# W_v's block differences: formed in advance through device memory, or in their places when these fall free

## The chip, the cores and the metric

The kernel runs on one core of one Trainium2 chip. The metric is the device time of one launch in microseconds (us), as the median of several runs. TensorE (PE in the profile; PEld its weight loads), VectorE (DVE), ScalarE (ACT), GpSimd (POOL) and SyncE (SP) work side by side, each through its own queue in order. SP, ACT and POOL also issue DMAs (SPq, ACTq, POOLq in the timelines).

## The reference

One pre-normed graph-attention layer on 2708 nodes with 1024 features, all in float32:

```
h   = relu(layernorm(x))
q   = h @ W_q.T + b_q;   k = h @ W_k.T + b_k;   v = h @ W_v.T + b_v
z   = (q @ k.T) / sqrt(1024) * adj            # adj: 0 or 1, about 4 ones in a row
z   = where(z == 0, -10000, z)
out = x + relu(softmax(z, axis=1) @ v)
```

## The kernel before

The weights of q and k are multiplied into one matrix first, so that a score is a row of h times a row of `h @ M`. Each node has few neighbours, so scores and sums go over gathered rows of h and not over whole rows of adj. W_v is applied last, to the weighted sums of h.

**Two big products, one after the other.** Both are [2708 x 1024] by [1024 x 1024]: first h by the joined matrix (the q units), then the weighted sums u by W_v (the o units). Rows come in 22 tiles of 128, two tiles in a *unit*. There are ten q units (numbers 0 to 9, the last is `last_q`) and ten o units from 10 on; one tile stays alone at the end. A unit is a 2 x 2 block product in seven block products instead of eight (`multiply`, L1063): on the right stand the 512 x 512 blocks of the matrix, three of them used as they are, and four differences. The blocks lie in `M[:, i, j]`, [128, 4, 512] each, and the differences in `T[:, 0..3]`, the same shape, inside the tile `wlow`:

```
T0 = M01 - M00    T1 = M11 - T0    T2 = M11 - M01    T3 = M10 - T1
```

The order of a unit's products on TensorE is: s2 T1, a12 M10, s4 M11, s3 T2, then for the next unit a11 M00 and s1 T0, then a22 T3. `M[:, 0, 1]` (M01) is used in differences alone. The left factors a and s are sums and differences of the unit's row blocks. For the o units VectorE turns the rows (L706) and makes s1 and s3 (L723, L743); GpSimd makes s2 and s4 (also L723). Each product is eight matmul records of 128x512 in the trace, about 3.4 us.

**Steps of a unit.** `after(i)`, i from 0 to 6, is called between the products of unit n; (n, i) names the place. What is written there is put into the program at that point. VectorE's queue keeps exactly this order from unit 4 (`FIRST`) on; the queues of ScalarE, SyncE and GpSimd are ordered by the framework's scheduler from then on. Each `after` also runs the attention stream a little further (`advance`).

**The attention stream** (`attention`) takes tile after tile. For a tile with K neighbours a row: GpSimd gathers K buffers of 128 rows of h (L611), each 128x1024; its query rows `pq` are loaded (L851, or gathered, L613); VectorE makes K scores (`junk`, L881); ScalarE takes the exponential; VectorE makes the weights (`coef`, `w`, `m`); ScalarE starts the sum `u` with the first buffer (L930, L921), VectorE adds the others (L941, L947), and each step frees its buffer for a later gather. The sum goes to `u_dram` (through `v`, L962) and comes back as rows `or` of an o unit (L701). Buffers are handed out from the list `free` in order. There are eleven buffers `slots` and, as two more, the place of M01. A gather leaves out the rows of missing neighbours, so a buffer must hold finite numbers before its first use.

**Where the results of a q unit go.** `q_results` copies or adds the banks into q (ScalarE L1107, L1118; VectorE L1113, L1110) and stores q (L1103). In an o unit the additions are L1144 and L1140.

**W_v's way in.** At (3, 4), `searched` loads W_v's four blocks into `slots[0..7]`, in sixteen pieces of 256 KB (L802). At (4, 1) and (4, 5), `ts_of_wv` forms the four differences with sixteen subtractions of 128x512 (L811 to L814) and stores them to `tv_dram` with sixteen DMAs (L816). At (4, 6) those eight buffers join the free list. In units 9 and 10, as each place falls free of the joined matrix, seven loads of 1 MB on SyncE's queue bring M00, T0, T1, M10, M11, T2 and T3 (L1335):

```
for k, at in enumerate(((0, 0), (0, 1), (0, 3), (0, 4), (0, 5), (0, 5), (1, 2))):
```

Each pair is (n - last_q, i).

## Time and profile before

| | |
|---|---|
| time, median of 3 runs | 655.42 us (654.75 to 655.88) |
| the profiled execution | 654.23 us, span 652.5 us |
| TensorE / VectorE busy | 631.6 us (97%) / 525.0 us (80%) |
| GpSimd / ScalarE busy | 403.1 us (62%) / 281.6 us (43%) |
| moved by DMA | 187.46 MB, 287 GB/s over the span |
| granted TensorE clock, mean | 0.991 |

A timeline row gives the start from the beginning of the span, the time taken (of a whole run of equal instructions, x their number), engine, line, operation, out<-in, the shape, and in brackets how long the engine stood idle before it and what ended that. A window row gives the busy time of each engine in a stretch, with the granted clock, the busy share of the DMA engines and their rate. `wlow` stands for a T, `M` for a block or, in a gather, for its use as a buffer; `psy`, `ps` are banks of results.

### The profile page before, as it was taken

The page shows a single profiled execution, that of the slowest core. Times are in us where ns is not written, and L with a number is a line of the kernel's source. Part 1 is how long each engine was busy: PE and PEld are TensorE (multiplying, and loading weights), DVE is VectorE, ACT ScalarE, POOL GpSimd, SP SyncE. Part 2 cuts the span into 40 slices and gives each one's busy share as a digit, 9 for nine tenths or more (in the row PEclk, how much of TensorE's full clock was granted, in tenths as well). Part 3 has the DMA queues.
Part 4 walks back from the last instruction along what each step waited for, and adds up shares of the span by engine and source line. Part 5 has one row for each costly group of instructions (what it writes and reads, how often), then busy time and mean ns, then how long its engine had stood idle before and what let it go on. Part 6 is the DMA issues. An engine that isn't in the chain of part 4 may idle for free.

```text
span 652.5 us, 6269 instructions
## 1 busy us (share of the span) xinstructions
PE 631.6 (97%) x1651; PEld 318.5 (49%) x1651; DVE 525.0 (80%) x988; ACT 281.6 (43%) x423; POOL 403.1 (62%) x415
## 2 busy tenths in 40 slices
PE   9999999999989999999999987999999999999994
PEld 5777766444434444444444432444444444444441
DVE  5999788998893754989879927999998898998521
ACT  3548974948495532434422132443233233342300
POOL 2549950976847677776752812677868787874421
PEclk9999999999999999999999997999999999999998
DMA  8998988597789969996799998999999989982551
GB/s 337 406 353 313 357 317 325 174 367 273 249 300 348 344 191 403 336 323 187 240 317 354 255 417 235 285 307 350 330 358 334 322 242 283 260 274 64 136 167 57
DMA packets 65089, 187.46 MB, mean 287 GB/s; under 512 B 10343, under 2 KB 15799, under 8 KB 64152
## 3 DMA queue, kind: packets, MB, share of 16 engines
q1 hardware_dynamic: 34410, 89.10, 39.6%
q0 software_dynamic: 25136, 78.41, 38.1%
q10 hardware_dynamic: 5502, 19.48, 7.6%
q8 instruction: 15, 0.25, 0.2%
q14 instruction: 26, 0.21, 0.1%
HBM read 151.94 MB, written 44.93 MB: 302 GB/s over the span
## 4 chain that ended last, share of the span: by engine, by line
PE 58%; DMA 13%; DVE 13%; issue 8%; POOL 4%; ACT 2%; another core or an unknown queue 0%; POOLq 0%; DVEq 0%; SPq 0%; ACTq 0%
PE ps L1029 23%; PE psy L1029 16%; DMA g<-h_dram,tab 7%; PE ps_y L477 6%; DVE u L941 5%; DVE junk L881 4%; PE ps_x L477 4%; PE ps_z L477 4%; PE pt L416 3%; DMA y<-in_x_dram,tab 2%; POOL g L611 2%; DMA h_dram<-x 2%; DMA qr<-h_dram,tab 1%; DMA M<-in_wv_dram 1%; ACT sized L369 1%
## 5 line engine op out<-in xcount | busy, mean ns | idle before, releaser
L1029 PE MATMUL psy<-wlow,s 128*128 128x512 f32 x320 | 144.2, 593 | 3.5 <-ACT psy L1042 1.9
L1029 PE MATMUL ps<-M,a 128*128 128x512 f32 x320 | 144.2, 593 | 0.5 <-ACT ps L761 0.5
L611 POOL DMA_INDIRECT g<-h_dram,tab x87 | 105.1, 1207 | 44.9 <-issue 18.0
L881 DVE SCALAR_TENSOR_TENSOR junk<-g,pq 128x1024 uint8<-128x1024 f32 x86 | 110.5, 1285 | 22.5 <-DMA pq<-q_late 14.4
L941 DVE SCALAR_TENSOR_TENSOR u<-g,coef,u 128x1024 f32<-128x1024 f32 x67 | 94.3, 1408 | 3.9 <-ACT u L930 2.4
L1029 PEld LDWEIGHTS psy<-wlow,s 128*128 128x128 f32 x320 | 59.3, 190 | 73.5 <-issue 68.6
L1029 PEld LDWEIGHTS ps<-M,a 128*128 128x128 f32 x320 | 59.6, 190 | 71.3 <-issue 68.1
L1029 PE MATMUL ps<-wlow,s 128*128 128x512 f32 x160 | 74.7, 611 | 4.5 <-DVE s L723 4.5
L390 DVE FIND_INDEX8 at<-ones,adj 128x8 uint32<-128x685 f32 (+1 forms) x88 | 74.5, 865 | 0.0
L1029 PE MATMUL ps<-M,s 128*128 128x512 f32 x160 | 72.0, 593 | 0.9 <-DMA M<-in_wv_dram 0.9
L1029 PE MATMUL psy<-wlow,a 128*128 128x512 f32 x160 | 71.9, 592 | 0.0
L369 ACT ACTIVATE sized<-adj 128x2708 uint8<-128x2708 f32 (+1 forms) x22 | 54.2, 2466 | 7.4 <-DMA adj<-in_adj_dram 6.1
L299 POOL TENSOR_TENSOR hsum<-hsum,x 128x256 f32<-128x256 f32 (+1 forms) x56 | 38.6, 730 | 27.4 <-DVE wlow L445 23.5
L1029 PEld LDWEIGHTS ps<-wlow,s 128*128 128x128 f32 x160 | 31.2, 196 | 44.9 <-issue 43.5
L1029 PEld LDWEIGHTS ps<-M,s 128*128 128x128 f32 x160 | 30.2, 190 | 39.3 <-issue 38.8
L1029 PEld LDWEIGHTS psy<-wlow,a 128*128 128x128 f32 x160 | 30.4, 190 | 38.3 <-issue 37.8
L1128 POOL DMA_INDIRECT y<-in_x_dram,tab x19 | 33.1, 1740 | 17.7 <-ACT y L1145 8.0
L723 POOL TENSOR_TENSOR s<-s,a 128x512 f32<-128x512 f32 x18 | 24.2, 1346 | 30.9 <-DVE s L723 30.7
L826 POOL DMA_INDIRECT out_dram<-y,tab x21 | 28.7, 1368 | 20.6 <-DMA y<-in_x_dram,tab 8.2
L930 ACT ACTIVATE u<-g,coef 128x1024 f32<-128x1024 f32 x15 | 17.2, 1150 | 37.6 <-DVE coef L929 33.5
L723 POOL TENSOR_TENSOR s<-a,s 128x512 f32<-128x512 f32 x18 | 29.6, 1646 | 1.2
L627 POOL DMA_INDIRECT tab_dram<-tab,pos_i x22 | 22.2, 1008 | 11.8 <-DVE pos_i L690 6.3
(254 smaller groups left out, 899.2 us busy)
## 6 DMA issues: line engine op xcount, KB each, us to landing
adj<-in_adj_dram SPq DMA_DIRECT2D x21, 1354.0 KB
x<-in_x_dram SPq DMA_DIRECT2D x21, 512.0 KB
h_dram<-x ACTq DMA_DIRECT2D x21, 512.0 KB
q_late<-q SPq DMA_DIRECT2D x12, 512.0 KB
pq<-q_late SPq DMA_DIRECT2D x12, 512.0 KB
u_dram<-v ACTq DMA_DIRECT2D x10, 512.0 KB
or<-u_dram SPq DMA_DIRECT2D x40, 128.0 KB
g<-in_wv_dram SPq DMA_DIRECT2D x16, 256.0 KB
```

The source lines that it names most:

```text
L299: small.append(nc.gpsimd.tensor_add(hsum[:n, cols], hsum[:n, cols], xt[:n, cols]))
L369: nc.scalar.activation(sized[:n], a[:n, :, :PW], AF.Abs, accum_out=total[:n, t:t + 1])
L390: nc.vector.max_index(at[:n, k - first_k, g, :], ones[:n, 0:8], a[:n, g, :])
L477: mm = nc.tensor.matmul(bank, a_tile(o + H * a[0], a[1], i), b(o), start=first and o == 0, stop=(o == H - 1), skip_group_check=True)
L611: return nc.gpsimd.indirect_dma_start(out=dst, out_offset=None, in_=src, in_offset=off, bounds_check=N - 1, oob_is_err=False)
L627: put = nc.gpsimd.indirect_dma_start(out=tab_dram[lo >= EARLY][:, :], out_offset=bass.IndirectOffsetOnAxis(ap=pos_i[:n, t:t + 1], axis=0), ...
L723: step = (eng or nc.vector).tensor_tensor(ops[name], a, b, op=op)
L826: to = nc.gpsimd.indirect_dma_start(out=out, out_offset=bass.IndirectOffsetOnAxis(ap=ptab.bitcast(U32)[:n, t, SLOTS:SLOTS + 1], axis=0), i ...
L881: chained(lambda: nc.vector.scalar_tensor_tensor(junk, g_of[t][s], 1.0, tq[t], op0=ALU.mult, op1=ALU.mult, accum_out=zall[:, t, s:s + 1]))
L941: chained(lambda: nc.vector.scalar_tensor_tensor(u, g_of[t][s], coef[:, s:s + 1], u, op0=ALU.mult, op1=ALU.add))
L1029: mm = nc.tensor.matmul(bank, a[:, c, :], b[:, c, :], start=False, stop=(c == 3), skip_group_check=True)
L1128: return nc.gpsimd.indirect_dma_start(out=y[:n], out_offset=None, in_=x, in_offset=off, compute_op=ALU.add)
```

## The change

The differences are no longer made in advance. `slots` are not loaded with W_v; at (4, 1) VectorE sets eight of them to zero (the other three are cleared on GpSimd as before), and all eleven join the free list before the first gathers. M01's place holds W_v's second block from (8, 0) on, and joins the free list, as two buffers, only at (10, 1). Five loads of 1 MB remain: M01 at (8, 0), M00 at (9, 0), the block M11 into T1's place at (9, 2), M10 at (9, 3) and M11 at (9, 4). Four subtractions of 128x2048 on VectorE make T0 at (9, 2), T1 in its own place at (9, 5), T3 at (10, 0) and T2 at (10, 1).

```diff
-    tv_dram = dram.tile([4, P, 4, NB], FT, name="tv_dram")
...
-        for c in range(4):
-            for k, (i, j) in enumerate(((0, 0), (0, 1), (1, 1), (1, 0))):
-                nc.sync.dma_start(slots[2 * c + k // 2][:, k % 2 * NB:(k % 2 + 1) * NB], wv[j][:, i * 4 + c, :])
         assert len(adj_loads) == NT
-        free.extend([M.rearrange("p i j (a c) w -> p i j a (c w)", a=2)[:, 0, 1, a, :] for a in range(2)] + slots[8:])
-
-    def ts_of_wv(lo, hi):
-        with tc.issue_after(behind[-1].ins), tc.issue_after(sorted_at[-1].ins):
-            for c in range(lo, hi):
-                b11, b12 = slots[2 * c][:, :NB], slots[2 * c][:, NB:]
-                b22, b21 = slots[2 * c + 1][:, :NB], slots[2 * c + 1][:, NB:]
-                nc.vector.tensor_sub(b11, b12, b11)
-                nc.vector.tensor_sub(b12, b22, b12)
-                nc.vector.tensor_sub(b22, b22, b11)
-                nc.vector.tensor_sub(b21, b21, b22)
-                for k, r in enumerate((b11, b22, b12, b21)):
-                    nc.sync.dma_start(tv_dram[k][:, c, :], r)
...
     def attention(order):
         for t in order[:2]:
             ask(t)
+        free.extend(slots)
...
         marked(0, EARLY)
-        free.extend(slots[:8])
-        fill()
...
-            if (n, i) in ((FIRST, 1), (FIRST, 5)):
-                ts_of_wv(i // 2, i // 2 + 2)
+            if (n, i) == (FIRST, 1):
+                for g in slots[:HIGH - 3]:
+                    nc.vector.memset(g, 0.0)
+            b11, b12, b21, b22 = M[:, 0, 0], M[:, 0, 1], M[:, 1, 0], M[:, 1, 1]
+            for at, place, src in (((-1, 0), b12, of_wv(0, 1)), ((0, 0), b11, of_wv(0, 0)), ((0, 2), T[:, 1], of_wv(1, 1)),
+                                   ((0, 3), b21, of_wv(1, 0)), ((0, 4), b22, of_wv(1, 1))):
+                if (n - last_q, i) == at:
+                    nc.sync.dma_start(place, src)
+            for at, place, a, b in (((0, 2), T[:, 0], b12, b11), ((0, 5), T[:, 1], T[:, 1], T[:, 0]),
+                                    ((1, 0), T[:, 3], b21, T[:, 1]), ((1, 1), T[:, 2], b22, b12)):
+                if (n - last_q, i) == at:
+                    nc.vector.tensor_sub(place, a, b)
+            if (n - last_q, i) == (1, 1):
+                free.extend(M.rearrange("p i j (a c) w -> p i j a (c w)", a=2)[:, 0, 1, a, :] for a in range(2))
...
-            for k, at in enumerate(((0, 0), (0, 1), (0, 3), (0, 4), (0, 5), (0, 5), (1, 2))):
-                if (n - last_q, i) == at:
-                    place, src = ((M[:, 0, 0], of_wv(0, 0)), (T[:, 0], tv_dram[0]), (T[:, 1], tv_dram[1]),
-                                  (M[:, 1, 0], of_wv(1, 0)), (M[:, 1, 1], of_wv(1, 1)), (T[:, 2], tv_dram[2]),
-                                  (T[:, 3], tv_dram[3]))[k]
-                    nc.sync.dma_start(place, src)
```

## The prediction

> **What bounds it now.** I read the page first, then the windows by stretch, then TensorE's timeline for its pauses, and the other engines' timelines around the longest pause.
>
> ```profile
> span 652.5 us, 6269 instructions
> PE 631.6 (97%) x1651; PEld 318.5 (49%) x1651; DVE 525.0 (80%) x988; ACT 281.6 (43%) x423; POOL 403.1 (62%) x415
> ...
> 187.00:205.00 18.00, 15.04 (x35) 6.19 (x33) 13.05 (x30) 13.96 (x16) 11.42 (x17) 1.00 1.02 387
> 205.00:230.00 25.00, 24.48 (x83) 12.81 (x84) 14.87 (x44) 13.78 (x26) 18.55 (x30) 1.00 0.91 317
> ...
> 376.00:400.00 24.00, 17.76 (x41) 7.23 (x40) 8.80 (x17) 5.96 (x11) 1.34 (x3) 0.96 1.03 386
> 400.00:410.00 10.00, 10.00 (x18) 4.30 (x19) 9.37 (x17) 4.15 (x9) 5.54 (x4) 0.75 0.61 140
> 410.00:434.00 24.00, 24.00 (x57) 10.61 (x57) 23.54 (x38) 9.91 (x16) 15.84 (x12) 1.00 1.02 302
> ```
>
> The page gives TensorE 631.6 of 652.5 us. The window rows (busy time of PE, PEld, DVE, ACT, POOL, then granted clock, DMA share, GB/s) say where the rest is. In 376 to 400 TensorE is busy 17.76 of 24 us and VectorE only 8.80, while the DMA engines are full (share 1.03, 386 GB/s); the next 10 us run at a granted clock of 0.75. From 410 on VectorE is busy 23.54 of 24 us. So TensorE sets the pace wherever its inputs are there, VectorE is just behind it, and this one hole is made by transfers. TensorE's timeline has its pauses:
>
> ```profile
> 193.34 3.70 PE L1029 MATMUL psy<-wlow,s 128*128 128x512 f32 x8 [1.87 <-ACT psy L1042]
> ...
> 205.52 1.06 PE L416 MATMUL pt<-ident,qr 128*128 128x128 f32 x8 [1.60 <-DMA qr<-h_dram,tab]
> ...
> 372.40 3.60 PE L1029 MATMUL psy<-wlow,a 128*128 128x512 f32 x8
> ...
> 383.77 3.67 PE L1029 MATMUL ps<-M,s 128*128 128x512 f32 x8 [0.91 <-DMA M<-in_wv_dram]
> 388.27 3.67 PE L1029 MATMUL psy<-wlow,s 128*128 128x512 f32 x8 [0.83 <-DMA wlow<-tv_dram]
> 391.78 3.60 PE L1029 MATMUL ps<-M,a 128*128 128x512 f32 x8
> 399.88 6.25 PE L1029 MATMUL ps<-wlow,s 128*128 128x512 f32 x8 [4.50 <-DVE s L723]
> ...
> 426.56 3.60 PE L1029 MATMUL ps<-wlow,s 128*128 128x512 f32 x8
> ```
>
> Four pauses lie in what the change touches: 1.60 at 205.52 for rows read back from h_dram, 0.91 at 383.77 for a block of W_v, 0.83 at 388.27 for a stored difference, and 4.50 at 399.88 for VectorE's s. The group after the last one takes 6.25 us where its neighbours take 3.60, so that pause costs 4.50 + 2.65 = 7.15 us. Why s was late stands in VectorE's timeline:
>
> ```profile
> 368.22 0.68 DVE L1110 TENSOR_TENSOR q<-psy,p 128x512 f32<-128x512 f32 x1
> ...
> 378.35 1.18 DVE L881 SCALAR_TENSOR_TENSOR junk<-M,pq 128x1024 uint8<-128x1024 f32 x1
> ...
> 379.46 1.28 DVE L941 SCALAR_TENSOR_TENSOR u<-g,coef,u 128x1024 f32<-128x1024 f32 x1
> 395.19 1.23 DVE L881 SCALAR_TENSOR_TENSOR junk<-g,pq 128x1024 uint8<-128x1024 f32 x1 [14.44 <-DMA pq<-q_late]
> ...
> 399.04 0.69 DVE L723 TENSOR_TENSOR s<-a,s 128x512 f32<-128x512 f32 x1
> ...
> 423.11 0.69 DVE L723 TENSOR_TENSOR s<-a,s 128x512 f32<-128x512 f32 x1
> ```
>
> VectorE ended its work at 380.74 (379.46 + 1.28), stood still for 14.44 us until the query rows pq of the next tile had landed, and only then came to s (395.19 to TensorE's restart at 399.88: 4.69 us). SyncE's queue shows what lay ahead of those rows:
>
> ```profile
> 345.37 0.37 SPq L1335 DMA_DIRECT2D M<-in_wv_dram  x1
> 348.56 0.32 SPq L1335 DMA_DIRECT2D wlow<-tv_dram  x1
> ...
> 355.43 0.32 SPq L1335 DMA_DIRECT2D wlow<-tv_dram  x1
> ...
> 367.11 2.64 SPq L1335 DMA_DIRECT2D M<-in_wv_dram  x2
> 370.57 0.33 SPq L1335 DMA_DIRECT2D wlow<-tv_dram  x1
> 371.23 7.99 SPq L1103 DMA_DIRECT2D q_late<-q  x2
> ...
> 379.32 0.44 SPq L851 DMA_DIRECT2D pq<-q_late  x1
> ```
>
> In order: M's first block, T0, T1, the third and fourth block, T2, two stores of q, and pq, issued at 379.32 and used at 395.19, 15.87 us later; T3 follows right behind. Seven transfers of 1 MB belong to W_v.
>
> **Part by part.** The costs come from these rows:
>
> ```profile
> g<-in_wv_dram SPq DMA_DIRECT2D x6, 256.0 KB
> ...
> wlow<-tv_dram SPq DMA_DIRECT2D x4, 1024.0 KB
> ...
> L812 DVE TENSOR_TENSOR g<-g,g x4: 691/691/692, 224.5 to 241.6; 128x512 f32<-128x512 f32 x4
> ...
> L445 DVE TENSOR_TENSOR wlow<-M x4: 1204/1218/1220, 93.0 to 113.0; 128x1024 f32<-128x1024 f32 x4
> ...
> L141 DVE MEMSET keys<- 128x352 f32 x1 | 0.4, 352 | 1.0 <-PEq L1558 1.0
> ```
>
> The early part, units 3 and 4. Sixteen loads of 256 KB and as many stores go. Six of the loads are issued from 187 to 205; at 387 GB/s these 1.57 MB are 4.1 us of the DMA engines' time, in the stretch in which TensorE waits 1.60 us for its rows. I take the whole 1.60 (bounds: 0, if those rows lose their time to the store of h_dram ahead of them, and 1.60). The sixteen small subtractions (0.69 us) go from VectorE, and eight memsets of 128x1024 come. No row has that shape; 128x352 takes 352 ns, so by proportion about 1.0 us each, 8 us in place of the 5.5 of the first eight subtractions. VectorE is busy 14.87 of 25 us there, so both are hidden; were they not, it would be 2.5 us.
>
> The gather buffers fall from 13 to 11 from unit 4 until unit 10, since M's fourth block now waits in its place. I price that at nothing in the forecast and return to it as a rival.
>
> Units 8 to 10. Of the seven 1 MB loads, T0, T2 and T3 are gone, T1's place takes a block of W_v instead, and the block that waits in M comes a unit earlier: four remain around the hole and one ahead of it. That one joins SyncE's queue behind unit 7's stores; it has no reader to wait for, since its place is no gather buffer any more. VectorE gets four subtractions of 128x2048. From 512 to 1024 columns the time grows by 1218 - 691 = 527 ns, so 2048 columns take about 1218 + 2 x 527 = 2.27 us, 9.1 in all. VectorE is on no spare time here, so all four move what comes behind them in its queue. T0's and T1's come before 378.35, T3's before the weights ahead of it, T2's just before the junk at 378.35. Their inputs: M's first block was issued at 345.37, T1's at 355.43, the third and fourth at 367.11, each over 10 us before the subtraction that needs it, so I count no wait (bound: 1 us for the last, for which TensorE itself waited 0.91). Behind T0's stands the addition of 368.22, which must read a bank before TensorE's group of 372.40 adds to it: it ends at 368.90 + 2.27 = 371.2, with 1.2 us to spare.
>
> Is a product held up? T0, T1 and T3 are ready ahead of theirs. T2 is ready at 378.35 + 4 x 2.27 = 387.4. Without its two small pauses TensorE would be there at 388.27 - 0.91 - 0.83 = 386.5, so it waits 0.9 and reaches s at 391.78 + 3.60 - 388.27 + 387.4 = 394.5.
>
> When does VectorE go on? It gets to the pq wait at 380.74 + 9.1 = 389.8. If pq still landed at 395.19 the subtractions would all fit in the old wait. With T2's megabyte gone from ahead of pq in the same queue it lands 1.05 MB / 386 GB/s = 2.7 us sooner, 392.5; with T0's and T2's both, 389.8. T0 was issued 31 us earlier and is long through, so I take 392.5 and keep 389.8 and 395.2 as ends. TensorE then restarts at 392.5 + 4.69 = 397.2, 2.7 us sooner, after a pause of 2.7 us in place of 4.50.
>
> The clock decides 2.65 us more. After the pause of 1.87 at 193.34 the next group took 3.70, after 4.50 it took 6.25. 2.7 is nearer to the first, so I count the 2.65 as gained. Then TensorE is 2.65 us nearer to VectorE: the next s ended at 423.80 (423.11 + 0.69) and was used at 426.56, 2.76 us later, which just covers it. [...]
>
> Sum: 1.60 + 2.7 + 2.65 = 6.9 us. The profiled execution took 654.23 us (its span and 1.73 around it) and becomes 647.3; the median shown is 655.42, 1.19 above it, so the prediction for a median is 648.5. With pq at 389.8 it is 9.6 us, 645.8.
>
> **The rivals.**
>
> ```profile
> 377.25 1.15 ACT L921 ACTIVATE u<-hsum,m 128x1024 f32<-128x1024 f32 x1 [0.80 <-DVE m L920]
> 378.30 0.57 ACT L1118 COPY q<-psy 128x512 f32<-128x512 f32 x1
> ...
> 380.78 1.04 ACT L962 COPY v<-u 128x1024 f32<-128x1024 f32 x1 [1.29 <-DVE u L941]
> 381.73 0.58 ACT L1073 COPY u<-psy 128x512 f32<-128x512 f32 x1
> ```
>
> *Queues behind the weights (slower).* ScalarE copies the last q (L1118, 378.30) behind u (L921), which needs VectorE's weights; SyncE stores that q and only then issues pq. T0's, T1's and T3's subtractions now come before those weights, so the copy, the store and pq's issue all move by 6.8 us, pq to 386.1. If it again took 15.87 us less the 2.7 of T2, it would land at 399.3, 4.1 us later than before; TensorE restarts at 404.0 at a low clock, and the time is 655.42 + 4.1 - 1.60 = 657.9. It decides for slower once pq takes over 395.19 - 386.1 = 9.1 us. For it: the order of those two queues in the trace. Against it: by 386 the third and fourth block have landed, so little is queued ahead; and both queues are ordered anew around the subtractions. [...]
>
> *The copy of u2 behind v (faster by less).* v (L962, 380.78) follows VectorE's u of 379.46, and u2 (L1073) stands behind it; TensorE may write that bank with T2's product only after u2. Moved by 9.1 us, v starts at 389.9 and u2 ends at 391.4. TensorE pauses 4.9 us from 386.5, loses 2.65 to the clock, and reaches s at 391.4 + 6.9 + 2.65 = 401.0 instead of 399.88, but without the slow group after: 1.5 gained, 3.1 in all, 652.3.
>
> *Two buffers fewer.*
>
> ```profile
> 292.47 1.93 POOL L611 DMA_INDIRECT g<-h_dram,tab  x1 [0.90 <-DVE u L941]
> ...
> 290.93 3.92 DVE L941 SCALAR_TENSOR_TENSOR u<-g,coef,u 128x1024 f32<-128x1024 f32 x3
> ...
> 301.54 1.22 DVE L881 SCALAR_TENSOR_TENSOR junk<-g,pq 128x1024 uint8<-128x1024 f32 x1
> ```
>
> The gather at 292.47 waits for a buffer that a step of u (1.31 us each, 3.92 for three) frees, and is used at 301.54, 9.1 us later and without a wait. Two buffers fewer put it two steps back, to 6.5 us, so VectorE would wait 2.6 us at most. If that still lasted in unit 9, the addition of 368.22 would end at 371.2 + 2.6 = 373.8, 1.4 us after 372.40: 649.9. Against it: 50 us lie between, in which VectorE can catch up.
>
> *No change.* The early wait stays, since the rows follow the h_dram store, and the loads that are left keep pq where it was, the subtractions filling the old wait: 655.4. The full DMA share speaks for it, three megabytes fewer against.
>
> **How the numbers follow.** Forecast 0.45, queues behind the weights 0.28, u2 behind v 0.11, two buffers 0.08, no change 0.08. A measurement of this kernel tells about 0.2%, 1.3 us, from no change. Faster: 0.45 + 0.11 + 0.08 = 0.64; same 0.08; slower 0.28. The range goes from 645.5 (pq at VectorE's arrival) to 658.0 (the slower rival at its price), which leaves out about half of that rival and a little below; the forecast's own range is 645.5 to 652.
>
> **What would show it.** Right: no pause before the transposes near 205; four subtractions of about 2.27 us; T2's product waiting about 1 us; VectorE's pq wait about 3 instead of 14.44 us; a pause before s under 3 us and a following group of 3.6 us. Wrong: pq issued after 384 and landing after 395, ScalarE's v or u2 as the releaser of TensorE, gather waits on VectorE between 250 and 345, or VectorE late through the units after 410, where it has 2.76 us to give.

## The result and the profile after

| | before | after |
|---|---|---|
| time, median (lowest to highest) of 13 runs each | 655.93 us (654.39 to 658.09) | 650.74 us (648.08 to 653.73) |
| the profiled execution, and its span | 654.23 us, 652.5 us | 648.94 us, 647.2 us |
| moved by DMA | 187.46 MB | 176.97 MB |
| granted TensorE clock, mean | 0.991 | 0.995 |

The ratio is 0.9927, with a 95% interval of 0.9906 to 0.9948: 0.7% faster by the ratio, and 5.2 us between the medians. Ratios here and below are worked out from all undisturbed runs, so they can differ a little from the quotient of two medians. In the kernel after, the lines have other numbers: before's L1029 is L1010, L1073 is L1054, L1094 is L1075, L881 is L863, L851 is L833, L701 is L700, L723 is L722; the new subtractions are L1263, the new loads L1259.

The page and the windows of the kernel after, to be laid beside those of the prediction (busy time of PE, PEld, DVE, ACT, POOL, then granted clock, DMA share, GB/s):

```profile
span 647.2 us, 6198 instructions
...
PE 628.8 (97%) x1651; PEld 317.6 (49%) x1651; DVE 529.4 (82%) x984; ACT 281.2 (43%) x423; POOL 412.8 (64%) x415
```

```profile
187.00:205.00 18.00, 16.20 (x44) 7.39 (x43) 13.05 (x29) 14.49 (x17) 10.17 (x15) 1.00 0.88 327
205.00:230.00 25.00, 25.00 (x79) 12.44 (x78) 15.32 (x44) 15.23 (x29) 19.65 (x31) 1.00 0.49 166
370.00:394.00 24.00, 21.77 (x50) 9.52 (x51) 23.12 (x34) 7.44 (x12) 15.97 (x10) 1.00 0.87 320
...
400.00:410.00 10.00, 9.76 (x24) 4.32 (x24) 9.79 (x18) 5.64 (x10) 8.02 (x6) 1.00 0.88 238
410.00:434.00 24.00, 24.00 (x57) 10.52 (x56) 23.57 (x38) 9.62 (x15) 15.79 (x10) 1.00 1.03 313
```

The hole is gone. In the 24 us from 370 TensorE is busy 21.77 and VectorE 23.12, where VectorE had stood at 8.80, and from 400 the granted clock is 1.00 instead of 0.75. The DMA share from 205 to 230 has fallen from 0.91 to 0.49. TensorE's timeline after, and, in a fence of its own, one row of its timeline before that the prediction did not show:

```profile
192.50 3.70 PE L1010 MATMUL psy<-wlow,s 128*128 128x512 f32 x8 [1.80 <-ACT psy L1023]
...
202.90 1.04 PE L415 MATMUL pt<-ident,qr 128*128 128x128 f32 x8
...
370.34 3.70 PE L1010 MATMUL psy<-wlow,a 128*128 128x512 f32 x8 [0.43 <-DVE q L1091]
...
386.23 3.67 PE L1010 MATMUL psy<-wlow,s 128*128 128x512 f32 x8 [1.89 <-DVE wlow L1263]
...
393.17 3.60 PE L1010 MATMUL ps<-wlow,s 128*128 128x512 f32 x8
...
417.69 3.60 PE L1010 MATMUL ps<-wlow,s 128*128 128x512 f32 x8
...
471.60 3.70 PE L1010 MATMUL psy<-wlow,a 128*128 128x512 f32 x8 [2.20 <-ACT taken L1075]
...
566.61 3.70 PE L1010 MATMUL psy<-wlow,s 128*128 128x512 f32 x8 [1.88 <-ACT u L1054]
```

```profile
571.99 3.70 PE L1029 MATMUL psy<-wlow,s 128*128 128x512 f32 x8 [0.80 <-ACT u L1073]
```

Equal groups stand in the same order in both kernels, so the difference of their starts is TensorE's lead. At the transposes it is 205.52 - 202.90 = 2.62 us, at a group behind the hole 426.56 - 417.69 = 8.87, at the last pause 571.99 - 566.61 = 5.38, and at the end of the span 5.3. So the profile of this pair says: 2.6 early, over 6 in the hole, and 3.5 given back, most of it at the new pause of 2.20 before 471.60 (ScalarE's `taken`) and the longer one before 566.61 (u2, 1.88 instead of 0.80). VectorE and SyncE in the hole, from the timeline of all engines:

```profile
354.46 2.29 DVE L1263 TENSOR_TENSOR wlow<-M 128x2048 f32<-128x2048 f32 x1 [1.79 <-DMA M<-in_wv_dram]
...
357.93 0.32 SPq L833 DMA_DIRECT2D pq<-q_late  x1
...
358.34 4.57 SPq L700 DMA_DIRECT2D or<-u_dram  x8
...
363.23 0.97 SPq L1259 DMA_DIRECT2D M<-in_wv_dram  x2
...
367.24 12.32 SPq L1084 DMA_DIRECT2D q_late<-q  x2
...
370.20 2.28 DVE L1263 TENSOR_TENSOR wlow<-wlow 128x2048 f32<-128x2048 f32 x1
...
377.56 2.28 DVE L1263 TENSOR_TENSOR wlow<-M,wlow 128x2048 f32<-128x2048 f32 x1
...
383.84 2.25 DVE L1263 TENSOR_TENSOR wlow<-M 128x2048 f32<-128x2048 f32 x1
...
388.35 1.22 DVE L863 SCALAR_TENSOR_TENSOR junk<-g,pq 128x1024 uint8<-128x1024 f32 x1
...
392.16 0.69 DVE L722 TENSOR_TENSOR s<-a,s 128x512 f32<-128x512 f32 x1
```

The four subtractions are there (2.25 to 2.29 us). The junk at 388.35 is the first that reads tile 17's pq, and it comes without a wait: the 14.44 us are gone. And that row's load is issued at 357.93, ahead of the loads of `or`, where it stood at 379.32 before. Nobody wrote that move; the scheduler that orders SyncE's queue made it. So three things could have closed the hole: fewer bytes ahead of pq, the earlier place of its load, and the subtractions that fill the wait.

### The profile page after: what moved, and what is told of

It is laid out like the page before. It is cut to its first block, busy times and chain, and to the rows that moved or that the text cites. A ratio compares the mean times of both kernels' runs of the same rounds, so it can differ in the third digit from the quotient of the medians.

```text
span 647.2 us, 6198 instructions
## 1 busy us (share of the span) xinstructions
PE 628.8 (97%) x1651; PEld 317.6 (49%) x1651; DVE 529.4 (82%) x984; ACT 281.2 (43%) x423; POOL 412.8 (64%) x415
## 2 busy tenths in 40 slices
DMA packets 60193, 176.97 MB, mean 273 GB/s; under 512 B 9799, under 2 KB 15255, under 8 KB 59512
## 4 chain that ended last, share of the span: by engine, by line
PE 57%; DVE 17%; issue 10%; DMA 7%; POOL 5%; ACT 2%; SPq 1%; POOLq 0%; DVEq 0%; ACTq 0%
PE ps L1010 22%; PE psy L1010 16%; PE ps_y L476 6%; DVE junk L863 6%; DVE u L923 5%; PE ps_x L476 4%; PE ps_z L476 4%; DMA g<-h_dram,tab 3%; PE pt L415 3%; DMA M<-in_wv_dram 2%; POOL g L610 2%; DMA adj<-in_adj_dram 1%; POOL y L1109 1%; POOL s L722 1%; DVE a L705 1%
## 5 line engine op out<-in xcount | busy, mean ns | idle before, releaser
L1010 PE MATMUL psy<-wlow,s 128*128 128x512 f32 x320 | 144.3, 594 | 5.8 <-DVE wlow L1263 1.9
L610 POOL DMA_INDIRECT g<-h_dram,tab x94 | 119.0, 1266 | 47.3 <-issue 18.6
L1010 PE MATMUL ps<-M,a 128*128 128x512 f32 x320 | 144.0, 593 | 0.0
L863 DVE SCALAR_TENSOR_TENSOR junk<-g,pq 128x1024 uint8<-128x1024 f32 x93 | 119.3, 1282 | 17.2 <-DMA g<-h_dram,tab 13.8
L923 DVE SCALAR_TENSOR_TENSOR u<-g,coef,u 128x1024 f32<-128x1024 f32 x70 | 100.6, 1438 | 5.1 <-ACT u L912 3.6
L1010 PEld LDWEIGHTS psy<-wlow,s 128*128 128x128 f32 x320 | 59.1, 190 | 76.6 <-issue 67.5
L1010 PEld LDWEIGHTS ps<-M,a 128*128 128x128 f32 x320 | 59.7, 190 | 70.4 <-issue 69.2
L1010 PE MATMUL psy<-wlow,a 128*128 128x512 f32 x160 | 72.1, 593 | 2.6 <-ACT taken L1075 2.2
L1010 PE MATMUL ps<-M,s 128*128 128x512 f32 x160 | 71.9, 592 | 0.0
L1010 PE MATMUL ps<-wlow,s 128*128 128x512 f32 x160 | 71.9, 592 | 0.0
L1010 PEld LDWEIGHTS psy<-wlow,a 128*128 128x128 f32 x160 | 30.2, 190 | 41.6 <-issue 37.3
L1010 PEld LDWEIGHTS ps<-wlow,s 128*128 128x128 f32 x160 | 30.3, 190 | 38.3 <-issue 36.8
L1010 PEld LDWEIGHTS ps<-M,s 128*128 128x128 f32 x160 | 30.3, 190 | 38.1 <-issue 37.8
L912 ACT ACTIVATE u<-g,coef 128x1024 f32<-128x1024 f32 x17 | 19.5, 1149 | 45.9 <-DVE coef L911 39.8
L722 POOL TENSOR_TENSOR s<-s,a 128x512 f32<-128x512 f32 x18 | 24.2, 1343 | 14.3 <-DVE s L722 14.1
L722 DVE TENSOR_TENSOR s<-a,pt 128x512 f32<-128x512 f32 x30 | 19.2, 682 | 16.7 <-ACT junk_m L375 5.6
L722 POOL TENSOR_TENSOR s<-a,s 128x512 f32<-128x512 f32 x18 | 30.1, 1674 | 1.3
```

What stands on the lines that cost most here:

```text
L610: return nc.gpsimd.indirect_dma_start(out=dst, out_offset=None, in_=src, in_offset=off, bounds_check=N - 1, oob_is_err=False)
L722: step = (eng or nc.vector).tensor_tensor(ops[name], a, b, op=op)
L863: chained(lambda: nc.vector.scalar_tensor_tensor(junk, g_of[t][s], 1.0, tq[t], op0=ALU.mult, op1=ALU.mult, accum_out=zall[:, t, s:s + 1]))
L912: nc.scalar.activation(u, g_of[t][0], AF.Copy, scale=coef[:, 0:1])
L923: chained(lambda: nc.vector.scalar_tensor_tensor(u, g_of[t][s], coef[:, s:s + 1], u, op0=ALU.mult, op1=ALU.add))
L1010: mm = nc.tensor.matmul(bank, a[:, c, :], b[:, c, :], start=False, stop=(c == 3), skip_group_check=True)
```

## The experiments

Twelve runs in three groups, each group on one chip with the kernel before beside it. Differences between kernels of one group are given with a 95% interval from the scatter of their runs, of the medians where the text says so and else of the means. The theory to test was that the place of the pq load closed the hole, and that VectorE then sets the pace and takes part of it back; the rivals were fewer bytes, fewer buffers, and chance.

| kernel | time, median (runs) | ratio to before, 95% |
|---|---|---|
| *group 1*, before: 651.18 us | | |
| after, again | 646.70 us (12) | 0.9933 (0.9905 to 0.9962) |
| before, pq early | 646.83 us (12) | 0.9941 (0.991 to 0.9973) |
| after, pq late | 647.63 us (12) | 0.9959 (0.9929 to 0.9988) |
| after, with the early loads | 647.50 us (12) | 0.9952 (0.9922 to 0.9982) |
| *group 2*, before: 652.02 us | | |
| before, again | 650.88 us (1) | |
| after, pq late, 2 MB more | 646.57 us (12) | 0.9937 (0.9906 to 0.9968) |
| after, no subtractions | 644.38 us (12) | 0.9897 (0.9867 to 0.9928) |
| after, T0 and T3 on GpSimd | 649.22 us (12) | 0.9965 (0.9935 to 0.9994) |
| *group 3*, before: 651.12 us | | |
| before, two buffers fewer | 652.90 us (12) | 1.0032 (1.0009 to 1.0055) |
| after, pq late, 2 MB more, no subtractions | 645.93 us (10) | 0.9924 (0.9897 to 0.9952) |
| after, two scaled rows on VectorE | 645.91 us (9) | 0.9913 (0.9879 to 0.9946) |
| before, pq early, two scaled rows on VectorE | 645.20 us (8) | 0.9923 (0.9892 to 0.9954) |

### Is the early gain the loads' doing?

The kernel after, unedited:

> The changed kernel once more, nothing edited, beside the three kernels of this group. Theory: TensorE has no pause before s near 400 us, the pq row of tile 17 is issued near 358 us, and the time is 0.9927 of the kernel before, 650.7 us to its 655.9; the profile again shows a lead of about 8.9 us at 400 us of which 3 to 4 us are given back by the end. Rival (the missing pause was chance): a pause of 1 us or more before s comes back in this profile.

It came out at 0.9933, and the pause before s stayed away. Next, the sixteen loads put back:

```
-            if (n, i) == (FIRST, 1):
-                for g in slots[:HIGH - 3]:
-                    nc.vector.memset(g, 0.0)
+        for c in range(4):                      # in searched(), as in the kernel before
+            for k, (i, j) in enumerate(((0, 0), (0, 1), (1, 1), (1, 0))):
+                nc.sync.dma_start(slots[2 * c + k // 2][:, k % 2 * NB:(k % 2 + 1) * NB], wv[j][:, i * 4 + c, :])
```

> The changed kernel with the 16 loads of W_v (4 MB) into eight buffers at the place where the kernel before has them, in place of the eight memsets; nobody reads what they bring. The prediction's step: the rows qr come 1.6 us later again, TensorE waits 1.60 us before its transposes near 205 us and is 2.6 us later there than in the changed kernel; by the end it costs 1.6 us, 652.3 us, ratio 0.995. Rival (later slack absorbs it, since after 400 us VectorE sets the pace): 2.6 us at 205 us and under 0.7 us at the end. Second rival (memsets are what costs): the time falls.

And the kernel before, unedited, for a second profile:

> The kernel before once more, for its profile. In the profiles of the first group the transposes near 205 us came without a wait for qr in two kernels that still have the 16 early loads of W_v, and with one of 0.73 us in one that has not. Theory 'loads' (the prediction's step): TensorE again waits 1.60 us for qr before the transposes near 205 us. Theory 'chance of one execution': no such wait, or one under 0.8 us, and TensorE reaches the transposes 2 us or more sooner than in the first profile, loads or not. In both the pause of about 4.5 us before s near 397 us, with the lower clock behind it, is there again.

TensorE's first group of transposes in that stretch, with the loads: first the kernel after that has them again, then the kernel before:

```profile
200.59 1.04 PE L415 MATMUL pt<-ident,qr 128*128 128x128 f32 x8
```

```profile
200.54 1.04 PE L416 MATMUL pt<-ident,qr 128*128 128x128 f32 x8
```

Both have the loads, and neither waits; both come to the transposes 5 us ahead of the first profile of before (205.52) and over 2 ahead of the kernel after (202.90). So do the others: the twelve profiles of the three groups stand between 200.31 and 201.91 there, with the loads or without. The 1.60 us is not the kernel's, and 'loads' falls for these groups. Whether it was the chance of one execution, or belongs to the session of the result, in which both profiles stand later, is not shown. On the clock of the whole kernel the loads cost 0.8 us at the median beside the kernel after, with an interval of the medians of about -0.9 to 3.0 that holds both 0 and 1.6.

### What closed the hole?

First the order alone, in the kernel before:

```
         tq.pop(t, None)
-        if then is not None:
+        if then is not None and then not in tq:
             fetch(then)
+        if t == BARE:
+            fetch(17)
```

> The kernel before, with one load moved: the pq row of tile 17 is asked for at the end of tile 20's scores instead of at the end of tile 7's, so that it stands on SyncE's queue behind the eight loads of or and ahead of M's second column (issue near 362 us instead of 379.32). Both loads of W_v and the stores between stay. Theory 'order': the hole before s is the place of that one load on SyncE's queue, so VectorE's wait of 14.44 us for pq is gone, TensorE does not pause 4.50 us before s and keeps its clock (2.65 us), and 2 to 4 us of these 7.15 are given back later as in the changed kernel: 652 to 654 us, ratio 0.994 to 0.997. Rival 'bytes': the ten megabytes that the change no longer moves are what lets pq land in time; then pq still lands after 385 us here and the time stays at 655 to 656.

```profile
390.21 1.23 DVE L881 SCALAR_TENSOR_TENSOR junk<-g,pq 128x1024 uint8<-128x1024 f32 x1 [14.48 <-DMA pq<-q_late]
...
394.90 5.34 PE L1029 MATMUL ps<-wlow,s 128*128 128x512 f32 x8 [4.50 <-DVE s L723]
```

```profile
361.65 0.34 SPq L851 DMA_DIRECT2D pq<-q_late  x1
...
390.65 3.60 PE L1029 MATMUL ps<-wlow,s 128*128 128x512 f32 x8
```

The first two rows are of the kernel before in its second profile: the wait (14.48 us), the pause (4.50) and the slow group (5.34, with 0.67 granted from 395 to 400) come back in every detail. The last two are of the edited kernel: pq issued at 361.65, the s group without a pause and at 3.60. One load moved ahead of five others (M10, M11, T2 and two stores of q), with every byte of W_v left as it was, gives 0.9941, as much as the whole change within the error. VectorE then waits 5.05 us for the next tile's row, at 395.01, but behind its s, where TensorE does not notice. 'Order' stands as sufficient. Is it needed? The kernel after, with pq back in its old place:

```
         elif t >= EARLY:
-            nc.sync.dma_start(tq[t], q_late[(t - EARLY) * P:(t - EARLY + 1) * P, :])
+            with tc.issue_after(stored[19].ins) if t == 17 else nullcontext():
+                nc.sync.dma_start(tq[t], q_late[(t - EARLY) * P:(t - EARLY + 1) * P, :])
```

> The changed kernel, with the pq row of tile 17 issued only behind the store of tile 19's q, where the kernel before has it (near 379 us). Nothing else is edited. The prediction's own step (fewer bytes ahead of it): pq lands near 392.5 us, 2.7 us sooner than before; VectorE, which reaches it near 388 us, waits 3 to 5 us, TensorE pauses less than 3 us before s without losing clock, and the time is 648 to 653 us, at most 2 us over the changed kernel. Theory 'order' (the early issue is worth the whole hole): a pause of 3 us or more before s with a lower clock behind it, 3 us or more over the changed kernel, ratio to the kernel before 0.997 to 1.001.

```profile
378.30 7.93 SPq L834 DMA_DIRECT2D pq<-q_late  x2
...
387.00 1.22 DVE L863 SCALAR_TENSOR_TENSOR junk<-g,pq 128x1024 uint8<-128x1024 f32 x1
```

It is not needed. Issued at 378.30, pq is there when VectorE reaches it at 387.00, and no pause follows. The landing takes at most 8.7 us where it took 15.9; the prediction's own step had allowed a gain of 2.7 us. The time is 0.9 us over the kernel after by the medians (their interval -0.5 to 2.8) and 1.3 by the means (0.1 to 2.5), so a small price of the late place is likely. So here the bytes decide, or the subtractions that bring VectorE to pq later. Taking the subtractions away tells them apart:

```
                 if (n - last_q, i) == at:
-                    nc.vector.tensor_sub(place, a, b)
+                    pass
```

> The changed kernel without its four subtractions: T keeps the differences of the weight before, so the four products with T are made from other numbers and only their time counts. pq of tile 17 goes late on SyncE's queue here, which by itself cost 0.9 us with an interval over zero. Theory 'VectorE sets the pace after 400 us': without the 9.1 us TensorE has no wait of 1.65 to 1.89 us for T's third block near 385 us and none of 2.2 to 2.8 us for taken near 470 us, and the end is 2.5 to 4 us sooner than the changed kernel, ratio 0.986 to 0.990. Rival 'the subtractions lie in slack', as the prediction had it: within 1 us of the changed kernel, ratio 0.992 to 0.995.

Adding two of the three lost megabytes:

```
+    ballast = dram.tile([2, P, 4, NB], FT, name="ballast")
...
+                    if at == (0, 4):            # behind the load of M11
+                        with tc.issue_after(got.ins):
+                            nc.sync.dma_start(ballast[0], of_wv(0, 0))
...
+            if t == 17:                         # behind the load of pq
+                with tc.issue_after(got.ins):
+                    nc.sync.dma_start(ballast[1], of_wv(0, 0))
```

> The changed kernel with the pq row of tile 17 issued late (as in the run with that edit alone, where it still landed before VectorE needed it), and with two more transfers of 1 MB each from W_v to a place in DRAM that nobody reads: one where the kernel before loads T's third block (behind M's second column), one where it loads the fourth (right behind pq). Theory 'bytes beside pq': pq takes 15 us or more from its issue again (in the kernel before 379.32 to 395.2), VectorE waits 5 to 8 us for it, TensorE pauses 2 us or more before s, and as VectorE also has the subtractions the end is 5 to 7 us later than in the run without the two transfers: 652 to 655 us on that chip's scale, ratio 1.000 to 1.008. Rival: the two transfers do not matter, pq lands in under 9 us, ratio 0.994 to 0.997.

And both edits in one kernel:

> The kernel with the late pq row and the two extra transfers of 1 MB, now also without the four subtractions (T keeps the differences of the weight before, so the four products with T are made from other numbers). Theory 'joint backlog': without the subtractions VectorE hands its buffers back sooner, more gathers stand in front of pq, and with the two megabytes the backlog near 380 us is 4 MB or more; pq takes 10 us or more from its issue, VectorE waits 8 us or more for it and TensorE pauses 1 to 3 us before s: ratio 0.991 to 0.996. Rival: the two megabytes matter as little as they did beside the subtractions; pq takes about 8 us, VectorE waits 6 to 7 us as in the run without subtractions, no pause, ratio 0.988 to 0.991.

In the kernel without subtractions nobody held pq back, but the scheduler issued it late again, at 374.07. Its row, then those of the kernel with two megabytes more and without subtractions:

```profile
382.20 1.23 DVE L863 SCALAR_TENSOR_TENSOR junk<-g,pq 128x1024 uint8<-128x1024 f32 x1 [6.71 <-DMA pq<-q_late]
```

```profile
384.41 1.23 DVE L863 SCALAR_TENSOR_TENSOR junk<-g,pq 128x1024 uint8<-128x1024 f32 x1 [8.34 <-DMA pq<-q_late]
...
389.09 3.67 PE L1010 MATMUL ps<-wlow,s 128*128 128x512 f32 x8 [0.58 <-DVE s L722]
```

And the gathers issued from 360 to 385 us, with the median from issue to landing at the end of the row, in the second profile of before and in the kernel after with pq late:

```profile
g<-h_dram,tab POOLq DMA_INDIRECT x9, 18.2
```

```profile
g<-h_dram,tab POOLq DMA_INDIRECT x9, 7.3
```

The same reading of the other kernels is in this table. Its second column counts the loads of M's and T's blocks, the 'use' is VectorE's first junk with tile 17's pq.

| | W_v, issued 340 to 385 us | subtractions | gathers land after | pq: issue to use | VectorE's wait |
|---|---|---|---|---|---|
| before, again | 7.3 MB | in advance | 18.2 us | 15.9 us | 14.48 us |
| after, pq late, 2 MB more, no subtractions | 6.3 MB | none | 13.2 us | 9.8 us | 8.34 us |
| after, no subtractions (pq late) | 4.2 MB | none | 10.2 us | 8.1 us | 6.71 us |
| after, pq late, 2 MB more | 6.3 MB | on VectorE | 9.3 us | at most 8.7 us | none |
| after, pq late | 4.2 MB | on VectorE | 7.3 us | at most 8.7 us | none |

Two things are to be read here. The whole stretch is a backlog: the gathers, on a queue of their own, land as late as what stands behind W_v's blocks on SyncE's (17.3 us in before with pq early, too). The backlog grows with the bytes: from 4.2 to 6.3 MB the gathers land after 13.2 us instead of 10.2 without subtractions, and after 9.3 instead of 7.3 with them. It is smaller with the subtractions, behind which VectorE hands its buffers back later: with two megabytes more, the gathers from 354 us on are issued 2.3 to 7.8 us later with subtractions than without. And with the subtractions gone 6.71 us of the old wait is back, but pq is used at 382.20, early enough: TensorE's s group follows without a pause. So neither the early place of pq nor the subtractions are needed to close the hole; what is left of the change, fewer bytes among it, does it too. Of the subtractions' 9.1 us, 6.7 lie in what is left of the wait.

Of the expectations, the one for the two megabytes beside the subtractions failed outright: 15 us and a pause were expected, neither came. Without the subtractions it half held: 8.34 us of wait as expected, a pause of 0.58 us instead of 1 to 3. Of the three megabytes by which the kernels differ these two runs put back two. By the landing of pq they are worth 1.7 us (9.8 instead of 8.1). The third is 2.5 us at the 0.42 MB per us that the windows show from 375 to 390 us (413 to 424 GB/s in the second profile of before), which does not explain the step from 9.8 to 15.9. So that fewer bytes alone close the hole is not shown. The two gather buffers differ as well; they were taken from the kernel before:

```
-        free.extend([M.rearrange(...)[:, 0, 1, a, :] for a in range(2)] + slots[8:])
+        free.extend(slots[8:])
...
+            if (n - last_q, i) == (1, 1):
+                free.extend(M.rearrange(...)[:, 0, 1, a, :] for a in range(2))
```

> The kernel before with the two gather buffers of M given out only at (last_q + 1, 1), as in the changed kernel, so that tiles 6 to 0 are gathered with eleven buffers; everything else stays. Theory 'backlog': near 380 us six megabytes wait in front of pq, and two rows of 0.5 MB fewer can be among them; pq lands up to 2.5 us sooner (1 MB at the 0.42 MB per us of that stretch), the pause before s falls from 4.5 to 2 or 3 us, ratio 0.995 to 0.999. Rival (the prediction's 'two buffers fewer'): VectorE waits longer for its gathered rows between 250 and 345 us and TensorE behind it, the pause before s stays, ratio 1.001 to 1.005.

```profile
374.97 0.43 SPq L851 DMA_DIRECT2D pq<-q_late  x1
...
376.35 5.40 PE L1029 MATMUL ps<-M,a 128*128 128x512 f32 x8 [1.86 <-DMA M<-in_wv_dram]
...
392.05 1.23 DVE L881 SCALAR_TENSOR_TENSOR junk<-g,pq 128x1024 uint8<-128x1024 f32 x1 [15.65 <-DMA pq<-q_late]
```

pq takes 17.1 us from 374.97, so the buffers are not in the backlog. They have a price instead: 1.0032, about 2 us, with an interval clear of 1. Where it is paid, the one profile does not show: VectorE waits 2.7 us in three pieces for gathered rows between 250 and 345 us, where the second profile of before has no such wait, but TensorE loses nothing there, and the pause for M's block at 376.35 can be chance. The wait of VectorE itself is not chance: every profile with eleven buffers has 1.8 to 3.6 us of it, and those with thirteen have at most 0.4. What else makes the step from 9.8 to 15.9 us stays open. From 355 to 370 the DMA engines moved 246 GB/s in the second profile of before and 331 GB/s in the kernel with two megabytes more and no subtractions, full in both (DMA share at least 1.01 in each 5 us). That is 1.3 MB less in 15 us, by estimate 3.0 us more of backlog at 0.42 MB per us, and with the 2.5 us of the third megabyte most of the 6.1 us. Why the rate is lower is not shown; the order of the W_v loads beside the small pieces of `or` is the next suspect, and was not tried.

### What is given back behind the hole?

The kernel without subtractions is also the test here. It came to 0.9897, 2 us better than the kernel after's 0.9927 and 0.9933, and 1.9 us (plus or minus 1.7) better than the kernel with two megabytes more beside it. It leaves the differences out, so its products with T are not the layer's and only its time counts. The same group of TensorE without subtractions and in that neighbour; then VectorE's waits from 400 to 580 us (us in total, times, longest) without subtractions and in the kernel after:

```profile
411.80 3.60 PE L1010 MATMUL ps<-wlow,s 128*128 128x512 f32 x8
```

```profile
413.93 3.60 PE L1010 MATMUL ps<-wlow,s 128*128 128x512 f32 x8
```

```profile
DVE junk L863 <- DMA g<-h_dram,tab: 4.2, 2, 3.8
DVE junk L863 <- DMA M<-h_dram,tab: 2.2, 1, 2.2
```

```profile
DVE junk L863 <- DMA g<-h_dram,tab: 3.6, 4, 1.5
DVE junk L863 <- DMA M<-h_dram,tab: 2.1, 1, 2.1
```

The subtractions' 2.1 us lie ahead of this group (413.93 - 411.80; the two kernels were within 0.1 us of each other at 360 us): the pause before T2's product, 1.31 us in the second kernel and 1.89 in the kernel after, is gone without them. Behind it nothing is gained. From this group to the end of the span the kernel without subtractions takes 642.3 - 411.80 = 230.5 us, its neighbour 642.7 - 413.93 = 228.8, the kernel after 647.2 - 417.69 = 229.5, the first profile of before 652.5 - 426.56 = 225.9, its second one 228.5. So the theory was half right: time is given back there, but the subtractions have no part in it. VectorE waits for gathered rows for 6.4 us without them and 5.7 in the kernel after, no longer than in the kernel before (6.4 and 8.9 in its two profiles). That a TensorE which comes sooner only runs into waits that VectorE had all along fits this, and is not shown. Of the 3.6 us between the kernel after and the first profile of before, 2.6 lie between the two profiles of before as well. Over all profiles the stretch takes 225.9 to 228.5 us in the three of the kernel before that have the hole, 229.5 in before with pq early, and 228.5 to 231.6 in the nine of the kernel after and its variants. Next, less VectorE work by way of GpSimd:

```
-                                    ((1, 0), T[:, 3], b21, T[:, 1]), ((1, 1), T[:, 2], b22, b12)):
+                                    ((1, 0), T[:, 2], b22, b12), ((1, 1), T[:, 3], b21, T[:, 1])):
                 if (n - last_q, i) == at:
-                    nc.vector.tensor_sub(place, a, b)
+                    (nc.gpsimd if at in ((0, 2), (1, 1)) else nc.vector).tensor_sub(place, a, b)
```

> The changed kernel with T's first and fourth difference formed on GpSimd, and the third formed before the fourth (at the places of each other). VectorE loses 4.6 us of work and its wait for M's first block. A subtraction of 128x2048 on GpSimd is estimated at 5.1 to 6.7 us, four times the 1.27 to 1.67 us of its 128x512 ones. Theory 'VectorE sets the pace after 400 us': the wait for T's third block near 385 us goes, taken near 470 us is waited for 1 to 2 us less, and the end is 1 to 2.5 us sooner than the changed kernel, ratio 0.989 to 0.992. Rival 'GpSimd cannot take it': the gathers behind the two subtractions are issued up to 6 us later, VectorE waits for g, and the time is the changed kernel's or 1 to 3 us more, ratio 0.993 to 0.998.

```profile
380.69 4.52 POOL L1263 TENSOR_TENSOR wlow<-M,wlow 128x2048 f32<-128x2048 f32 x1
380.71 4.53 DVE L899 SCALAR_TENSOR_TENSOR m<-w,m 128x1 f32<-128x1 f32 x1 [0.46 <-ACT w L898]
...
385.85 1.15 ACT L903 ACTIVATE u<-hsum,m 128x1024 f32<-128x1024 f32 x1 [4.69 <-DVE m L902]
...
386.91 0.56 ACT L1054 COPY u<-psy 128x512 f32<-128x512 f32 x1
...
387.52 6.60 PE L1010 MATMUL psy<-wlow,s 128*128 128x512 f32 x8 [4.50 <-ACT u L1054]
```

2.6 us slower than its neighbour with two megabytes more (plus or minus 1.7). Neither theory had the reason. While GpSimd's subtraction runs from 380.69 to 385.21, a step of VectorE on one column, otherwise 0.16 us, takes 4.53 and ends with it. The other subtraction on GpSimd shows the same: it takes 4.50 us from 352.69, and a step of VectorE on one column that starts at 352.79 takes 4.42, where it takes 0.15 in the kernel after. Why the step lasts as long as the subtraction is not shown. The weights come late, ScalarE starts u late (385.85), u2's copy stands behind it, and TensorE pauses 4.50 us and goes on at a low clock (a group of 6.60, with 0.66 granted from 385 to 395). That is the prediction's rival 'copy of u2 behind v' by another road.

The two pauses that grew behind the hole are before `taken` and u2. In both, ScalarE's queue stands at the first scaled row of u, waiting for VectorE's coef, and the copy that TensorE needs is behind it. In the kernel after:

```profile
469.93 1.15 ACT L912 ACTIVATE u<-g,coef 128x1024 f32<-128x1024 f32 x1 [1.26 <-DVE coef L911]
470.98 0.57 ACT L1075 COPY taken<-psy 128x512 f32<-128x512 f32 x1
...
564.94 1.15 ACT L912 ACTIVATE u<-g,coef 128x1024 f32<-128x1024 f32 x1 [3.69 <-DVE coef L911]
```

So that row goes to VectorE for tiles 11 and 9:

```
-            nc.scalar.activation(u, g_of[t][0], AF.Copy, scale=coef[:, 0:1])
+            if t in (11, 9):
+                chained(lambda: nc.vector.tensor_scalar(u, g_of[t][0], coef[:, 0:1], None, op0=ALU.mult))
+            else:
+                nc.scalar.activation(u, g_of[t][0], AF.Copy, scale=coef[:, 0:1])
```

> The changed kernel with the first scaled row of u formed on VectorE instead of ScalarE for two tiles, 11 and 9. In the profiles ScalarE stands at that step (near 470 and 565 us) waiting for VectorE's coef, and TensorE's taken and u2 stand behind it on ScalarE: pauses of 2.20 to 2.83 us and of 1.88 to 2.84 us. Theory: both pauses go or shrink to under 1 us, VectorE pays 1.28 us each and saves its 1.2 us wait for ScalarE, and the end is 2 to 4 us sooner than the changed kernel, ratio 0.987 to 0.991. Rival: VectorE is late there anyway and TensorE waits for it two steps further on: ratio 0.992 to 0.995.

> The kernel before with the pq row of tile 17 early and, as in the run above, the first scaled row of tiles 11 and 9 on VectorE. Here only the pause near 562 us (2.78 us, with a lower clock behind it that cost 1.7 us) can go. Theory: 2 to 4 us sooner than the kernel with the early pq row alone, ratio 0.986 to 0.991. Rival: TensorE waits for VectorE's u two steps on instead: ratio 0.993 to 0.996.

```profile
522.16 3.70 PE L1010 MATMUL ps<-wlow,s 128*128 128x512 f32 x8 [1.59 <-ACT ps L760]
```

In the change, the pauses of 2.20 and 1.88 us are gone; one of 1.59 at 522.16, where ScalarE fills a bank late, has come. In the kernel before with pq early the pause of 2.78 us is gone, but its profile has one of 3.22 us at 377.80, for a block of W_v, that its parent's has not. From the group above to the end the two kernels take 228.5 and 225.6 us, where their parents took 229.5 and 231.6 (the change) and 229.5. The ratios are 0.9913 and 0.9923, about 1 us better than 0.9927 to 0.9941 and short of the 2 to 4 us expected, with intervals that overlap. These are the lowest ratios of versions that compute the whole layer; that they beat the change is likely and not shown.

## Why the prediction was right, and where it was not

It forecast 648.5 us; the median is 650.74, faster and inside the range. The range of 645.5 to 658.0 held no change as well, and part of the slower rival, so that says little. The side came out as argued: the hole was made by a late pq, and with it gone TensorE keeps its clock (1.00 from 400 to 410, where it was 0.75). The sum came out only in part. Step by step:

- *1.60 us early, for the loads gone.* Failed. Of the other profiles, none with the loads has a wait for qr there, and two without them have one, of 0.73 and 0.83 us. The step took the wait of one profile as the kernel's.
- *Memsets and subtractions.* 0.912 us for a memset where 1.0 was estimated, and 2.25 to 2.29 us for a subtraction where 2.27 was. Held.
- *No wait for their inputs (bound 1 us).* M00 came 1.79 us late for T0's subtraction: its load, issued at 342.71, took 11.7 us to 354.4. The addition behind it, given 1.2 us to spare, came 0.43 us late for TensorE (370.34). Mis-sized by 1.6.
- *T2's product waits 0.9.* It waited 1.89, mis-sized by 1.0: TensorE was there at 384.34 (386.23 - 1.89), 2.2 before the 386.5 of the sum, which had left out the lead from earlier on, and T2 was ready at 386.1, only 1.3 before the sum's 387.4.
- *pq lands 2.7 us sooner, for T2's megabyte.* The side is right, the size wrong, and the cause shown in part. With pq in its old place it landed at least 7.2 us sooner (at most 8.7 instead of 15.9). The step counted one block in one queue; the runs show a backlog of the whole stretch, over several queues. Two of the three megabytes are worth 1.7 us of it; the rest is in part open. In the kernel itself the load had also moved up by 21 us, which the prediction saw only as a danger ('both queues are ordered anew').
- *The clock, 2.65 us.* Gained: no pause before s, no slow group. The argument for it, an estimate from the pauses of 1.87 and 4.50 that one of 2.7 us keeps the clock, was not put to the test there, and the pauses of 2.19 and 2.78 us in the last section speak against it. Together with the 4.50 that is 7.15 us instead of the 5.35 forecast; on TensorE's timeline, 8.87 - 2.04 = 6.83.
- *VectorE's 2.76 us of slack just cover it.* Failed: of 8.87 us of lead 5.4 were left, after the pauses at `taken` and u2, behind VectorE's coef. How much of that is the change's stays open, as the two profiles of before differ by 2.6 us in this stretch themselves. The prediction's list named 'VectorE late through the units after 410' as a wrong sign, and it came.
- *Rivals.* 'Queues behind the weights' fell: ScalarE's copy of q now stands ahead of u on its queue (378.62 and 382.74), and the two stores of q end at 367.24 + 12.32 = 379.56, 0.34 us after the 379.22 of before and not 6.8. 'Copy of u2 behind v' fell here and came with the subtractions on GpSimd. 'Two buffers fewer' is real, about 2 us in the kernel before, and hidden in the sum; its sign, gather waits on VectorE between 250 and 345, came in the kernel after with 3.1 us (0.4 in before), where at most 2.6 was allowed.

So 6.9 was forecast as 1.6 + 5.3. What the runs bear out is 6.8 from the hole, less 0.6 for the pauses ahead of it (2.62 - 2.04) and 1.0 to 3.6 given back behind it (229.5 - 228.5 and 229.5 - 225.9), with nothing sure early; the medians of the two sessions say 5.2 and 4.5 us. That the total came so near is in part luck: the hole gave more than forecast, the early gain was not borne out, some was given back, and the load of pq moved up without anybody's plan.

## What to carry to other kernels

Before you price a transfer by what stands ahead of it on its own queue, look at how long its neighbours take to land: if all of them take 18 us for half a megabyte, as the gathers did in the second profile of before, the whole stretch is behind, and what one load needs is not told by its own queue. Here the earlier issue of one load closed the hole, and so did the change with that load at its old place. Take a second profile of the kernel before, before you count a wait of one or two microseconds as the kernel's. And when a hole closes, ask which engine is next: work that fills a wait is free only up to the wait that is left (here 6.7 of the subtractions' 9.1 us).

## What the runs showed of the hardware

The clock after a short pause is not settled by its length. Two pauses are shown above: 1.86 us in before with two buffers fewer (376.35), with a group of 5.40 behind it, and 2.20 us in the kernel after (471.60), with one of 3.70. Three more, of the kernel after with the early loads, of before with pq early, and of the kernel after in its second profile:

```profile
469.37 5.40 PE L1010 MATMUL psy<-wlow,a 128*128 128x512 f32 x8 [2.19 <-ACT taken L1075]
```

```profile
561.97 5.40 PE L1029 MATMUL psy<-wlow,s 128*128 128x512 f32 x8 [2.78 <-ACT u L1073]
```

```profile
566.72 3.70 PE L1010 MATMUL psy<-wlow,s 128*128 128x512 f32 x8 [2.84 <-ACT u L1054]
```

1.86, 2.19 and 2.78 us were followed by groups of 5.40, a loss of 1.7 to 1.8; 2.20 and 2.84 by 3.70. In the windows behind the first three the granted clock falls to 0.50 (378 to 380, 470 to 472, 564 to 566); behind the other two it is 1.00 (471 to 478, 566 to 570). What decides is not shown: no run here moved a pause to test it.

Where TensorE stands at 205 us differs between profiles by as much as the effect measured here: 205.52 and 200.54 in two of the kernel before. Most of it lies in three pauses ahead, of 0.49, 1.87 and 1.60 us, which the second profile does not have. The two profiles of the result's session are the late ones (205.52 and 202.90); the twelve of the groups stand between 200.31 and 201.91, whatever the kernel, and the kernel before also had a median of 655.93 us in that session and of 651.12 to 652.02 in the groups. So the session or its chip is a likelier cause than the single execution, and neither is shown. These kernels can be told apart only by many runs beside each other.
